# A list scheduler's port model: shorter holds for small GpSimd operations, later readers of loads

## The chip, the cores and the metric

The kernel runs on one core of a Trainium2 chip. The metric is the device time of one execution in microseconds. In the text PE is TensorE, DVE is VectorE, ACT is ScalarE, POOL is GpSimd and SP is the engine whose queue issues most transfers.

## The reference

A stack of four residual graph layers works on x of shape (128, 64, 256) with one 64x64 adjacency matrix, all in float32. Each layer takes a layer norm and a ReLU of its input.

```python
h = jnp.maximum(_layernorm(x, axis=-1), 0.0)
x = x + _L0_gnn_ref(h, adj, ...)   # two graph convolutions, then four LSTMs over windows of 1 to 4 nodes
h = jnp.maximum(_layernorm(x, axis=-1), 0.0)
x = x + _L1_gnn_ref(h, adj, adj, ...)   # spectral convolution, attention in 4 heads, MLP, three layer norms
h = jnp.maximum(_layernorm(x, axis=-1), 0.0)
x = x + _L2_gnn_ref(h, adj, ...)   # graph attention
h = jnp.maximum(_layernorm(x, axis=-1), 0.0)
x = x + _L3_gnn_ref(h, adj, ...)   # U (relu(U^T h W1 + b1)) W2 + b2, U the eigenvectors of the Laplacian
...
deg = jnp.sum(A, axis=0) + jnp.sum(A, axis=1) - jnp.diagonal(A)
L_norm = d_inv_sqrt[:, None] * L * d_inv_sqrt[None, :]
_, U = jnp.linalg.eigh(L_norm)
```

Layer 1 also needs the largest eigenvalue of its Laplacian.

## The kernel before

The 8192 rows (128 graphs of 64 nodes) are cut into tiles of 128 rows. Layer 0 takes eight groups of eight tiles; the LSTMs do most of TensorE's work, most of their products by a seven-product scheme for 2x2 blocks, whose sums of blocks GpSimd and VectorE make (`pieces`). Its results are stored to memory (`put`). Layers 1 to 3 take sixteen groups of four tiles, which are loaded from `put` one by one and stored to the output.

Beside this, the eigenvectors are computed on the core itself (`eig_decomp`, group `EIG`, its data in the tile `arena`): 62 Householder steps with 64x1, 64x64 and 64x128 operations, mostly on VectorE, each with one square root on GpSimd and, from the sixth step on, one broadcast of a matrix row by a transfer of SP's queue; then nine sweeps of multisection with 64x42 products (32 steps a sweep), a twisted factorisation, and repair of split blocks. The layers with index 1 to 3 need the result in layer 3.

Nothing of this order is written by hand. The code records every operation through proxies (`Plan.record`) with a price (`Plan.cost`: how long the engine is taken, and the latency until others may read). `Plan.schedule` then plans all engines together: again and again it picks for each engine the operation that can start first, by rank among those that are ready, and issues the earliest. The ranks of the main groups come from the group and the length of the path that follows; operations of `EIG` have the last rank on VectorE and ScalarE, and the first on TensorE and GpSimd. A value gets its buffer when its first operation is picked. `Plan.issue` emits the instructions in this order, so each engine runs its queue in the order planned, and real waits are semaphores that follow from the dependences. The planned times themselves appear nowhere on the chip.

Two parts of the plan matter here.

- **The port.** Operations marked `op.port` share one variable: all of GpSimd's, and VectorE's whose operands are all in SBUF, bar the layer norm's statistics and the reductions. Such an operation isn't planned to start before `port`, and sets it to the end of its own planned time.
- **Readiness.** When an operation is planned, those that depend on it become ready at its end plus latency, and a slack for another engine (0.05 us, for TensorE 0.12 or 0.4). A transfer of SP's queue is priced at its bytes over 390 GB/s, at least 0.6 us, with 2.2 us more until its readers may start.

`ln_stats` is the layer norm: for four tiles, eight statistics operations on VectorE, then four operations of four elements a partition on GpSimd: add epsilon, the power -0.5, a product, and a change of sign. ScalarE reads the two rows as scale and bias.

Of the kernel before, what the change touches and what calls it, by code (L numbers as in the profile page):

```python
# [8 lines left out]
ALU = mybir.AluOpType  # L9
# [59 lines left out]
class Plan:  # L69
# [44 lines left out]
    def record(self, eng, name, args, kw):  # L114
        op = self.run
        if op is None:
            op = Op(eng, name, args, kw, self.group)
            op.lead = self.lead
            if self.behind:
                op.deps.add(self.behind)  # L120
        else:
            op.calls.append((name, args, kw))
        aps = [(a, i == 0) for i, a in enumerate(args) if self.is_ap(a)]
        aps += [(a, k in ("out", "accum_out")) for k, a in kw.items() if self.is_ap(a)]
        for a, write in aps:
            ap = a.ap if isinstance(a, Virt) else a
            if str(ap.space) == "DRAM" and not self.tc.is_my_tile(ap.tensor):
                continue
            key = ap.tensor.name
            if isinstance(a, Virt):  # L130
                key = id(a.val)
                op.vals[a.val] = True
            step, count = ap.ap[0]
            p0, f0 = (ap.offset // step, ap.offset % step) if step else (0, ap.offset)
            ends = [s * (n - 1) for s, n in ap.ap[1:]]
            region = (p0, p0 + count, f0 + sum(min(e, 0) for e in ends), f0 + sum(max(e, 0) for e in ends) + 1)
            if isinstance(a, Virt) and a.val.kind in ("bank", "seed"):
                op.deps |= {o for o in a.val.users if o.eng != eng}
                a.val.users.append(op)
            reads, writes = self.seen.setdefault(key, ([], []))  # L140
            for log in (reads, writes) if write else (writes,):
                for r, o in log:
                    if o is not op and r[0] < region[1] and region[0] < r[1] and r[2] < region[3] and region[2] < r[3]:
                        op.deps.add(o)
                        if log is writes:
                            op.late.add(o)
                if write:
                    log[:] = [(r, o) for r, o in log if not (
                        region[0] <= r[0] and r[1] <= region[1] and region[2] <= r[2] and r[3] <= region[3])]
            (writes if write else reads).append((region, op))  # L150
        if eng == "PE":

            val = args[0].val
            if val.last and val.last is not op:
                op.deps.add(val.last)
            val.last = op
        if op is self.run:
            return self.link(op)
        flat = [a.ap if isinstance(a, Virt) else a for a, _ in aps]
        op.cost, op.lat = self.cost(op, flat)  # L160

        op.port = eng == "G" or (eng == "V" and not name.startswith("bn_") and "reduce" not in name
                                 and all(str(ap.space) == "SB" for ap in flat))
        op.index = len(self.ops)
        self.ops.append(op)
        self.link(op)
        if self.whole:
            self.run = op
# [9 lines left out]
    @staticmethod  # L178
    def cost(op, aps):

        def free(ap):
            n = 1
            for _, c in ap.ap[1:]:
                n *= c
            return n
        n = max(free(a) for a in aps)
        if op.name == "dma_start" and op.eng != "SP":
            return 0.6, 4.0
        if op.eng == "PE":
            n = free(aps[0])  # L190
            if op.name == "transpose":
                c = 0.11
            elif aps[0].ap[0][1] <= 64 and aps[1].ap[0][1] <= 64:
                c = 0.08
            else:
                c = 0.001672 * n + 0.006 if n >= 128 else 0.2
            return c, c + 0.22
        if op.eng == "V":
            if op.name == "bn_stats":
                c = 0.33  # L200
            elif op.name == "bn_aggr":
                c = 0.09
            elif op.name in ("tensor_copy", "tensor_scalar") and all(str(a.space) == "SB" for a in aps):
                c = 0.075 + 0.0006 * n + 0.05 * (len(aps) - 2)
            elif op.name == "reciprocal":
                c = 0.075 + 0.0065 * n
            elif op.name == "tensor_reduce" and aps[1].ap[-1][0] != 1:
                c = 0.075 + 0.0022 * n
            else:
                c = 0.075 + 0.00105 * n  # L210
            if "accum_out" in op.kw:
                c += 0.075
            return c, c + 0.12
        if op.eng == "ACT":
            c = 0.07 + 0.00082 * n + 0.1 * max(0, len(aps) - 2)
            if op.kw.get("func", op.args[2] if len(op.args) > 2 else None) is AF.Exp:
                c += 0.12
            return c, c + 0.15
        if op.eng == "G":
            c = 0.44 + 0.14 * n if op.kw.get("op") is ALU.pow else 0.12 + 0.00218 * n  # L220
            return c, c + 0.05
        c = max(0.6, free(aps[0]) * aps[0].ap[0][1] * 4e-6 / 0.39)
        return c, c + 2.2
# [6 lines left out]
    def schedule(self):  # L230
# [19 lines left out]
        table, order, span, port, many = None, [], 0.0, 0.0, False  # L250
        while len(order) < len(self.ops):
            oldest = min(left)
            best = None
            for e, ops in ready.items():
# [3 lines left out]
                for op in ops:  # L258
                    if op.group != self.aside and op.group >= oldest + self.window(oldest) + (op.eng == "SP"):
                        continue  # L260
                    t = max(now[e], op.ready, port) if op.port else max(now[e], op.ready)
# [4 lines left out]
                    for k, c in need.items():  # L266
# [4 lines left out]
                        t = max(t, times[c - 1]) if len(times) >= c + spare else None  # L271
# [12 lines left out]
            _, t, op = best  # L284
            e = op.eng
            ready[e].remove(op)
            tb = self.table(op)
            cost, lat = op.cost, op.lat
            if tb and tb != table:
                table, cost, lat = tb, cost + 1.29, lat + 1.29  # L290
            if e == "PE" and op.many != many:
                many, cost, lat = op.many, cost + 0.178, lat + 0.178
            now[e] = t + cost
            if op.port:
                port = t + cost
            end = t + lat
            for v in op.vals:
                if v.buf is None:
# [10 lines left out]
            for o in op.after:  # L309
                o.wait -= 1  # L310
                if o.eng != e:
                    o.ready = max(o.ready, end + self.slack(o))
                else:
                    o.ready = max(o.ready, end - 0.01 if op in o.late and e != "PE" else t + cost)
                if not o.wait:
                    ready[o.eng].append(o)
# [1495 lines left out]
```

## Time and profile before

| | |
|---|---|
| median of three runs | 2116.32 us (2113.99 to 2117.18) |
| the profiled execution | 2117.02 us, span 2115.2 us |
| busy: TensorE, VectorE, ScalarE, GpSimd | 2072.3, 1767.0, 1094.7, 756.6 us |
| statistics of layer norms on GpSimd: powers of 128x4 | 110, mean 1101 ns |
| transfers of 512 KB from the input, issue to landing | 29, median 5.0 us |
| granted TensorE clock | 0.997 |

Nearly all instructions carry line L347, that of the call in `Plan.issue`, so the profile is read by engine, tile and shape. Tiles keep their names without numbers: `big`, `mids`, `stat`, `bank` and `seed` (the last two in PSUM) are pools; `arena`, `sums`, `Wih` and `Whh` hold eigenvalue data or weights first and serve as more buffers later. A busy time is the union of an engine's instructions; those of TensorE overlap and their ends are modelled. A wait names the engine whose semaphore came last.

### The profile page before, as it was taken

Reading aid. Unit: us, or ns where it says so; the run is one execution under the profiler, and the core shown is the slowest. Engines: PE = TensorE matmul, PEld = TensorE weight load, DVE = VectorE, ACT = ScalarE, POOL = GpSimd, SP = SyncE. Lnnn points to the kernel's source line nnn. Section 1 sums busy time; section 2 is a strip of 40 time slices with the busy share of each in tenths; the row PEclk is TensorE's granted clock in tenths of the full one; section 3 lists DMA queues with packets and bytes.
Section 4 is the critical chain, followed back from the end, with each engine's and each line's share of the span. In section 5 each row is a group of like instructions: output and inputs, shape, how many; then the busy total and the mean of one; then the engine's idle time right before and its main releaser. Section 6 shows DMA issues by size and latency. Waiting matters only on the chain.

```text
span 2115.2 us, 48093 instructions
## 1 busy us (share of the span) xinstructions
PE 2072.3 (98%) x17924; PEld 1675.9 (79%) x17924; DVE 1767.0 (84%) x6669; ACT 1094.7 (52%) x2451; POOL 756.6 (36%) x1144
## 2 busy tenths in 40 slices
PE   8999999999999999999999999999999999999997
PEld 6688689688788788788788789877778778877775
DVE  7788888889999999999988956868779699885785
ACT  3344544534543543543444345666666567575763
POOL 6522212222201201201100215685467658663452
PEclk9999999999999999999999999999999999999999
DMA  6000100100100100100000211100000000000001
GB/s 229 1 3 13 52 3 2 62 2 2 60 1 1 61 1 2 46 1 10 32 1 21 90 49 35 62 1 22 22 21 22 21 22 22 22 2 11 1 12 51
DMA packets 44875, 57.83 MB, mean 27 GB/s; under 512 B 8929, under 2 KB 38497, under 8 KB 44641
## 3 DMA queue, kind: packets, MB, share of 16 engines
q1 hardware_dynamic: 43536, 53.71, 7.9%
q8 instruction: 141, 2.31, 0.5%
q10 hardware_dynamic: 1104, 1.05, 0.2%
q14 instruction: 94, 0.76, 0.1%
HBM read 37.53 MB, written 16.78 MB: 26 GB/s over the span
## 4 chain that ended last, share of the span: by engine, by line
PE 80%; DVE 13%; issue 2%; ACT 2%; POOL 2%; DMA 0%; SPq 0%; ACTq 0%; DVEq 0%; POOLq 0%
PE bank L347 64%; PE seed L347 16%; DVE arena L347 5%; DVE big L347 4%; DVE stat L347 2%; ACT mids L347 1%; DVE mids L347 1%; POOL stat L347 1%; DVE sums L347 1%; POOL big L347 1%; ACT big L347 0%; DMA arena<-put 0%; DVE bank L347 0%; POOL sums L347 0%; DVE seed L347 0%
## 5 line engine op out<-in xcount | busy, mean ns | idle before, releaser
L347 PE MATMUL bank<-big,Wih 128*128 128x512 f32 (+4 forms) x1802 | 554.5, 424 | 2.9 <-DVE big L347 1.9
L347 PEld LDWEIGHTS bank<-big,Wih 128*128 128x128 f32 x1802 | 314.7, 190 | 145.5 <-issue 95.5
L347 PE MATMUL bank<-big,sums 128*128 128x128 f32 (+3 forms) x2328 | 375.7, 289 | 5.2 <-DVE seed L347 2.5
L347 ACT ACTIVATE mids<-bank,bl 128x512 f32<-128x512 f32 (+2 forms) x432 | 247.2, 576 | 214.3 <-PE bank L347 195.2
L347 PEld LDWEIGHTS bank<-big,sums 128*128 128x128 f32 (+1 forms) x2328 | 298.5, 180 | 42.8 <-issue 19.6
L347 PE MATMUL bank<-big,Whh 128*128 128x128 f32 (+3 forms) x1294 | 312.3, 327 | 0.0
L347 DVE TENSOR_TENSOR arena<-arena 64x42 f32<-64x42 f32 (+6 forms) x1358 | 276.5, 231 | 18.4 <-POOL arena L347 1.2
L347 PEld LDWEIGHTS bank<-big,Whh 128*128 128x128 f32 x1294 | 214.0, 191 | 18.5 <-issue 10.5
L347 ACT ACTIVATE mids<-seed,bl 128x256 f32<-128x256 f32 (+2 forms) x192 | 102.0, 531 | 217.0 <-PE seed L347 209.0
L347 DVE TENSOR_TENSOR big<-mids 128x512 f32<-128x512 f32 (+2 forms) x256 | 151.1, 597 | 27.1 <-ACT mids L347 17.1
L347 POOL TENSOR_SCALAR stat<-stat 128x4 f32<-128x4 f32 (+1 forms) x228 | 68.4, 301 | 281.1 <-DVE stat L347 268.9
L347 PE MATMUL seed<-big,sums 128*128 128x128 f32 (+3 forms) x896 | 143.3, 291 | 0.0
L347 DVE SCALAR_TENSOR_TENSOR arena<-arena 64x1 f32<-64x1 f32 (+15 forms) x565 | 136.1, 264 | 4.5 <-POOL arena L347 1.0
L347 POOL TENSOR_TENSOR big<-big 128x128 f32<-128x128 f32 (+2 forms) x55 | 32.9, 600 | 294.6 <-DVE big L347 151.7
L347 POOL TENSOR_TENSOR stat<-stat,mhalf 128x4 f32<-128x4 f32 (+1 forms) x114 | 123.9, 1087 | 4.8
L347 ACT COPY seed<-bank 128x128 f32<-128x128 f32 (+2 forms) x192 | 54.0, 281 | 135.8 <-PE bank L347 128.5
L347 ACT ACTIVATE mids<-big 128x256 f32<-128x256 f32 (+2 forms) x176 | 89.5, 511 | 66.3 <-DVE big L347 62.1
L347 ACT COPY mids<-bank 128x256 f32<-128x256 f32 (+3 forms) x290 | 94.8, 352 | 51.9 <-PE bank L347 51.5
L347 PEld LDWEIGHTS seed<-big,sums 128*128 128x128 f32 (+1 forms) x896 | 118.4, 183 | 3.5 <-issue 0.3
L347 DVE TENSOR_SCALAR arena<-arena 64x1 f32<-64x1 f32 (+10 forms) x506 | 100.4, 206 | 7.8 <-POOL arena L347 0.5
L347 DVE TENSOR_TENSOR big<-big,mids 128x256 f32<-128x256 f32 (+2 forms) x196 | 99.0, 509 | 7.0 <-ACT mids L347 6.0
L347 PE MATMUL bank<-Wih,big 128*128 128x256 f32 x408 | 104.8, 383 | 0.0
(517 smaller groups left out, 4480.4 us busy)
## 6 DMA issues: line engine op xcount, KB each, us to landing
big<-in_x_dram SPq DMA_DIRECT2D x29, 512.0 KB, 5.0
put<-big SPq DMA_DIRECT2D x15, 512.0 KB, 3.2
big<-put SPq DMA_DIRECT2D x8, 512.0 KB, 6.4
out_dram<-big SPq DMA_DIRECT2D x16, 256.0 KB, 2.6
Wih<-in_WihT_dram SPq DMA_DIRECT2D x3, 1024.0 KB, 11.4
Whh<-in_WhhT_dram SPq DMA_DIRECT2D x3, 1024.0 KB, 12.9
arena<-put SPq DMA_DIRECT2D x3, 512.0 KB, 5.9
sums<-put SPq DMA_DIRECT2D x3, 512.0 KB, 4.3
```

What stands on the lines that cost most here:

```text
L347: getattr(self.engines[op.eng], name)(*map(real, args), **{k: real(a) for k, a in kw.items()})
```

## The change

Three edits, all in the planner. An operation with an operand of more than one free dimension, or with more than 64 elements in it, is wide and holds the port for its whole planned time as before; any other holds it for 0.06 us at most. GpSimd operations of up to 64 elements, bar the power, are priced at 0.2 us. An operation that depends on a transfer of SP's queue, on whatever other engine, is ready 1.5 us later.

```diff
         op.port = eng == "G" or (eng == "V" and not name.startswith("bn_") and "reduce" not in name
                                  and all(str(ap.space) == "SB" for ap in flat))
+        wide = max(ap.ap[-1][1] if len(ap.ap) == 2 else 65 for ap in flat) > 64
+        op.hold = op.cost if wide else 0.06
...
         if op.eng == "G":
-            c = 0.44 + 0.14 * n if op.kw.get("op") is ALU.pow else 0.12 + 0.00218 * n
+            c = 0.44 + 0.14 * n if op.kw.get("op") is ALU.pow else 0.12 + 0.00218 * n if n > 64 else 0.2
             return c, c + 0.05
...
             now[e] = t + cost
             if op.port:
-                port = t + cost
+                port = t + min(cost, op.hold)
...
                 if o.eng != e:
-                    o.ready = max(o.ready, end + self.slack(o))
+                    o.ready = max(o.ready, end + self.slack(o) + (1.5 if e == "SP" else 0.0))
```

The ranks, the windows of groups and the buffers' reserves stay as they are.

## The prediction

> **What bounds the kernel now.** I read the busy table first, then the chain that ended last, then the same busy times cut into stages (columns: stretch, its length, busy time of each engine with its instructions).
>
> ```profile
> PE 2072.3 (98%) x17924; PEld 1675.9 (79%) x17924; DVE 1767.0 (84%) x6669; ACT 1094.7 (52%) x2451; POOL 756.6 (36%) x1144
> PE 80%; DVE 13%; issue 2%; ACT 2%; POOL 2%; DMA 0%; SPq 0%; ACTq 0%; DVEq 0%; POOLq 0%
> ```
>
> ```profile
> 0.00:50.00 50.00, 44.33 (x515) 30.13 (x516) 39.39 (x165) 17.55 (x37) 34.91 (x62) 0.93 0.70 242
> 50.00:1150.00 1100.00, 1095.72 (x7573) 885.74 (x7573) 985.39 (x4305) 499.49 (x1281) 211.75 (x379) 1.00 0.06 18
> 1150.00:1350.00 200.00, 193.91 (x1585) 170.80 (x1587) 143.99 (x491) 95.07 (x231) 60.44 (x95) 1.00 0.20 62
> 1350.00:2050.00 700.00, 690.75 (x7475) 549.53 (x7466) 554.79 (x1575) 458.39 (x857) 428.34 (x577) 1.00 0.05 14
> 2050.00:2115.20 65.20, 47.61 (x798) 39.71 (x797) 43.46 (x136) 24.16 (x48) 21.20 (x33) 0.95 0.15 50
> ```
>
> TensorE bounds it everywhere but in the last 65 us. Its idle time is 5.7 us at the start, 4.3 in layer 0, 6.1 in the change of layers, 9.3 in the three later layers and 17.6 at the end: 42.9 in all. Matmul ends are modelled, so I also took the distances between the starts of neighbouring matmuls (median 429 ns for 512 columns, 216 for 256, 143 for 168, 112 for 128) and added up what exceeds them: 89 us, of which 13 before 50 us, 19 to 1150, 37 to 2050, 20 in the tail. No change of order can give more than the 76 us outside the start; VectorE has 348 us idle and can only help through those.
>
> **What the planner believed, and what the trace shows.** The planner let one variable, the port, keep VectorE's SBUF operations and GpSimd's operations apart for the whole planned length of either. The trace shows three things on that.
>
> ```profile
> L347 POOL TENSOR_SCALAR stat<-stat x228: 213/229/1378, 6.9 to 2097.3; 128x4 f32<-128x4 f32 x110, 128x2 f32<-128x2 f32 x4
> L347 POOL TENSOR_TENSOR stat<-stat,mhalf x114: 696/1037/1859, 7.2 to 2095.9; 128x4 f32<-128x4 f32 x110, 128x2 f32<-128x2 f32 x4
> L347 POOL TENSOR_TENSOR stat<-stat x114: 188/199/661, 8.0 to 2097.0; 128x4 f32<-128x4 f32 x110, 128x2 f32<-128x2 f32 x4
> ```
>
> ```profile
> 1419.98 1.38 POOL L347 TENSOR_SCALAR stat<-stat 128x4 f32<-128x4 f32 x1
> 1420.01 1.27 DVE L347 TENSOR_TENSOR big<-big,stat 128x512 f32<-128x512 f32 x2
> ```
>
> ```profile
> 666.20 1.38 DVE L347 TENSOR_TENSOR arena<-arena 64x42 f32<-64x42 f32 x4
> 666.67 1.27 POOL L347 TENSOR_TENSOR big<-big,big 128x128 f32<-128x128 f32 x3
> ```
>
> The first three rows are durations in ns (minimum, median, maximum) of the four small operations of every layer norm. In the second view two 512-wide VectorE products run beside a small GpSimd one in 1.27 us together, as fast as ever, and it is GpSimd's 229 ns operation that takes 1378. In the third, beside wide GpSimd operations, the 64x42 product takes 0.35 us on average where it takes 0.19 alone. Over the whole trace: a 512-wide product from SBUF to SBUF has a median of 681 ns with GpSimd idle and 679 ns inside a small power (41 of them); the 64x42 product 190 ns alone, 189 inside a small power, 470 inside a wide operation. So a small GpSimd operation does not delay VectorE, a wide one does, and VectorE does delay the small ones.
>
> The Trainium skill, page "SBUF — State Buffer", section "Who interferes with whom", says that a VectorE instruction with two SBUF inputs contends with a GpSimd one that reads SBUF, and that whoever comes first holds the pair for the whole instruction. The wide rows here agree; the small ones don't: 679 ns beside a power of 1037 ns is no hold. "Perfetto Trace Analysis", section "Identifying the Most-Contended Engine", warns that matmul busy time is a poor measure and names weight-load time; that is 79% here, which agrees with my counting distances. No page prices the power or these small operations; the rows above do.
>
> **The change, part by part.** No instruction, transfer or semaphore is added or removed. Only planned times change, hence the order within each engine's queue, and which buffer a value gets.
>
> *Holds.* Before, one layer norm's four operations were planned at 0.129 + 1.0 + 0.129 + 0.129 = 1.39 us of port (0.12 + 0.00218 n, and 0.44 + 0.14 n for the power). 110 of these are 153 us. The 65 powers of the eigenvalue stage at 0.58 are 38 us, its 60 small memsets at 0.12 are 7: 198 us. After, 0.06 each: 440 + 65 + 60 operations, 34 us. The planner believes 164 us more of the port. A hold costs only where VectorE had nothing else to do: small GpSimd operations last 268 us in the trace, and VectorE was busy in 205 of them, so 63 us of its 348 idle us (18%) lie beside them. As an upper end I give this share of the 76 us that TensorE loses outside the start: 13.7. Some of this idle time waits for TensorE or ScalarE anyway (the rows of waits on VectorE name them nearly always), so I take half, **7 us**; the lower end is 0. Below nothing is the slower rival.
>
> *Prices.* Small GpSimd operations go from 0.129 to 0.2 (measured medians 229 and 199), a chain from 1.39 to 1.6 planned against 229 + 1037 + 199 + 229 = 1.69. Readers on ScalarE are planned 0.2 us later; ScalarE waits for these chains 87 us in all but is 48% idle. The small memset goes from 0.12 to 0.2 though it takes 0.093. Cover: ScalarE's idle time; if gone, 0.2 us times the three chains of the tail, 0.6 us. I take 0.
>
> *Loads.* Every operation on another engine that depends on a transfer of SP's queue is planned 1.5 us later.
>
> ```profile
> big<-in_x_dram SPq DMA_DIRECT2D x29, 512.0 KB, 5.0
> big<-put SPq DMA_DIRECT2D x8, 512.0 KB, 6.4
> ```
>
> Half a megabyte was planned at 1.34 + 2.2 = 3.5 us and takes 5.0 to 6.4; it becomes 5.0. The only wait of VectorE for a load that shows is 1.6 us in its row of statistics from arena. So the gain is at most 1.6 us plus part of the 13 at the start, the loss at most 1.5 us where the first readers are put behind something else. The same 1.5 us reaches the 57 row broadcasts of the eigenvalue stage (and the writers of the matrix that they read): planned 0.6 + 2.2 = 2.8 us, measured 2.1, now 4.3. Their iterations are 7.9 us apart in the trace (109.5 to 554.1 us for 56), so 4.3 still hides; were an iteration to depend on it alone, 56 x 1.5 = 84 us of planned time would move that stage later, into the stretch after 1150 where VectorE is 72% busy. On SP's queue nothing passes anything of weight: it idles until the buffers it loads into come free. I take **0**, with -2 to +2.
>
> *Sum.* 2117.0 us (the profiled execution: span 2115.2 and 1.8 around it) - 7 = 2110. The median of the runs is 2116.3, 0.7 lower: **2109**.
>
> **Rivals.** *Nothing within 0.2%.* (0.2%, 4 us, is about what a measurement of this kernel can tell from no change; the three runs spread over 3.2.) TensorE is 98% busy and its queue only shuffles. For it: between 50 and 1150 us only 19 us are lost at all, and of the first half megabytes all but a few are loaded far ahead. It gives 2116.
>
> *Slower: the released room is filled with eigenvalue work in front of TensorE's next input.* The hold was also a reserve, since the planner's prices for VectorE are low.
>
> ```profile
> L347 DVE TENSOR_TENSOR arena<-arena 64x42 f32<-64x42 f32 x855 | 140.3, 205 | 7.2
> L347 DVE SCALAR_TENSOR_TENSOR arena<-arena 64x1 f32<-64x1 f32 x269 | 60.4, 233 | 3.8 <-POOL arena L347 1.0 <-issue 0.2
> ```
>
> The 64x42 product is planned at 0.075 + 0.00105 x 42 = 0.119 and takes 0.205 on average, which alone hides 74 us. Between 50 and 1150 us, 61 powers (35 us) and 12 layer norms (17 us) release 52 us of port; the planner fills them with eigenvalue operations, which have VectorE's lowest rank. VectorE is 90% busy there and takes its queue in order: each one too many stands before a gate product, behind it ScalarE's tanh and TensorE's next step. If half of the 52 us do so and half of that reaches TensorE, 13 us: 2129. Against it: TensorE loses so little in this stretch that it has cover of several steps. It decides once TensorE's lost time between 50 and 1150 grows from 19 to over 26, more than the 7 gained.
>
> *Slower by a little: the block turned round.* Beside two-input VectorE work the small operations take 477, 1234 and 414 ns on average (63, 35 and 23 of them), against 229, 1036 and 199 elsewhere; a chain so covered takes 2.6 us instead of today's mean of 301 x 2 + 1101 + 244 = 1.95. More VectorE work beside them means more of this: 0.65 us on each of the tail's three bare chains and on some groups before, 2 to 5 us: 2120.
>
> *It doesn't do what it says.* The test of 64 elements looks at every port operation, VectorE's own 64x1 and 64x64 ones too; they then hold GpSimd off for 0.06 instead of 0.08 to 0.14 us. That is no more than 0.1 us an operation in the plan and would leave 2116.
>
> **How the numbers follow.** Forecast, with its larger variants (up to 13.7 + 2, and the tail of 17.6 idle us, where reordering can move some 8 either way): 0.48. Nothing, by either reason: 0.24. Slower through the eigenvalue work 0.20, through the chains 0.08. A changed order moves every later choice, so signs are uncertain although each price is small. The range goes from 2116 - 13.7 - 2 - 8 = 2092 to 2129 + 2 = 2131, leaving 1 in 10 out at each end. The likeliest case's own range is 2098 to 2114.
>
> **What would show it.** Right: the same instruction counts and 98 to 99% TensorE; idle beside small GpSimd operations below 63 us; TensorE's idle time in 1150 to 2050 below 15.4 and in the tail below 17.6; the small stat operations' means up a little. Slower rival: TensorE idle in 50 to 1150 above 4.3 with waits for DVE big, seed or mids. Wrong altogether: a new wait on a load, the eigenvalue stage ending later than 1200 us with later layers waiting for it, or a changed tail outweighing all the rest.

## The result and the profile after

The changed kernel takes 2108.25 us (2106.31 to 2109.63, six runs) against 2116.32: a ratio of 0.9961, with 0.9948 to 0.9974 as its 95% interval, 8 us or 0.4% faster. The profiled execution took 2106.31 with a span of 2104.5.

The busy table and the chain of the changed kernel, to lay beside those of before:

```profile
PE 2063.7 (98%) x17924; PEld 1676.3 (80%) x17924; DVE 1771.8 (84%) x6669; ACT 1095.0 (52%) x2451; POOL 775.8 (37%) x1144
...
PE 85%; DVE 10%; ACT 2%; issue 1%; DMA 1%; POOL 0%; DVEq 0%; ACTq 0%; SPq 0%
```

The engines' instruction counts are those of before; TensorE is busy 8.6 us less for the same 17924 matmuls: delays that do not count as idle time have gone. The same stages as before (the last one ends with the span; the last three numbers of a line are the granted TensorE clock, the DMA share and GB/s):

```profile
0.00:50.00 50.00, 42.70 (x508) 28.88 (x508) 36.78 (x156) 17.11 (x38) 37.62 (x64) 0.93 0.70 242
50.00:1150.00 1100.00, 1093.50 (x7564) 885.45 (x7557) 996.73 (x4344) 498.28 (x1277) 218.16 (x374) 1.00 0.06 17
1150.00:1350.00 200.00, 195.34 (x1490) 172.06 (x1489) 139.06 (x460) 95.61 (x233) 60.69 (x97) 1.00 0.21 67
1350.00:2050.00 700.00, 692.80 (x7679) 557.01 (x7678) 561.16 (x1609) 464.55 (x869) 440.93 (x584) 1.00 0.05 15
2050.00:2104.50 54.50, 39.40 (x701) 32.87 (x700) 38.09 (x105) 19.43 (x38) 18.36 (x27) 0.99 0.17 56
```

Idle time of TensorE is 7.3, 6.5, 4.7, 7.2 and 15.1 us, 40.8 in all: only 2.1 less. The better measure is the one of the prediction, the distances between the starts of matmuls beyond their medians. It fell from 88.8 us to 79.1: at the start 13.0 to 14.0, in layer 0 19.0 to 20.3, to 2050 us 36.7 to 29.7, in the tail 20.1 to 15.1. That is 9.7 of the 10.7 us between the two spans. In all kernels below, the span less this lost time lies between 2025.1 and 2027.7 us. All have the same matmuls, so this is nearly bookkeeping: it says in which stage the time went, not why.

A part of the lost time is TensorE's clock. The traces record stretches of 3.4 or 6.8 us with a granted clock of 0.5, and matmuls of one size start in them 1.98 times as far apart as elsewhere (median). Up to the last matmul, the kernel before has 12.5 us of such stretches and the changed one 6.8; the distances within them exceed the medians by about 6.1 and 2.7 us, so some 3.4 of the 9.7 us are there, most of it in the tail: 5.7 us of such stretches before, none after.

Between 50 and 1150 us VectorE is busier by 11.3 us, and the last row broadcast of the eigenvalue stage leaves at 527.3 us instead of 554.1. The layer norm's small operations:

```profile
L349 POOL TENSOR_SCALAR stat<-stat x228: 222/231/1186, 4.5 to 2087.6; 128x4 f32<-128x4 f32 x110, 128x2 f32<-128x2 f32 x4
L349 POOL TENSOR_TENSOR stat<-stat,mhalf x114: 721/1038/2110, 4.8 to 2086.2; 128x4 f32<-128x4 f32 x110, 128x2 f32<-128x2 f32 x4
L349 POOL TENSOR_TENSOR stat<-stat x114: 191/202/1179, 5.7 to 2087.3; 128x4 f32<-128x4 f32 x110, 128x2 f32<-128x2 f32 x4
```

Medians are within 3 ns of those before. Of 273 us of small GpSimd operations VectorE now leaves 47 unused (before: 63 of 268). All this looks like the prediction's mechanism at work, and every sign that the prediction named for its forecast came true: this idle time fell below 63 us, TensorE's idle time between 1150 and 2050 from 15.4 to 11.9 and in the tail from 17.6 to 15.1, and the means of the small operations rose a little. The experiments show that these signs don't credit the mechanism with the time.

### The profile page after: what moved, and what is told of

The parts are those of the page before. It is cut to its first block, busy times and chain, and to the rows that moved or that the text cites. A ratio compares the mean times of both kernels' runs of the same rounds, so it can differ in the third digit from the quotient of the medians.

```text
span 2104.5 us, 48069 instructions
## 1 busy us (share of the span) xinstructions
PE 2063.7 (98%) x17924; PEld 1676.3 (80%) x17924; DVE 1771.8 (84%) x6669; ACT 1095.0 (52%) x2451; POOL 775.8 (37%) x1144
## 4 chain that ended last, share of the span: by engine, by line
PE 85%; DVE 10%; ACT 2%; issue 1%; DMA 1%; POOL 0%; DVEq 0%; ACTq 0%; SPq 0%
PE bank L349 69%; PE seed L349 16%; DVE big L349 3%; DVE arena L349 3%; DVE stat L349 2%; DVE sums L349 1%; DVE mids L349 1%; ACT mids L349 1%; DMA big<-in_x_dram 1%; ACT big L349 0%; DVE seed L349 0%; POOL stat L349 0%; ACT arena L349 0%; ACT sums L349 0%; ACT L349 0%
## 5 line engine op out<-in xcount | busy, mean ns | idle before, releaser
L349 PE MATMUL bank<-big,Wih 128*128 128x512 f32 (+4 forms) x1776 | 545.7, 425 | 1.1 <-DVE big L349 0.7
L349 PE MATMUL bank<-big,sums 128*128 128x128 f32 (+3 forms) x1904 | 360.4, 303 | 5.8 <-DVE big L349 2.5
L349 PEld LDWEIGHTS bank<-big,sums 128*128 128x128 f32 (+1 forms) x1904 | 285.4, 189 | 40.7 <-issue 17.7
L349 PEld LDWEIGHTS bank<-big,Whh 128*128 128x128 f32 x1274 | 210.4, 191 | 20.7 <-issue 9.8
L349 PE MATMUL seed<-big,sums 128*128 128x128 f32 (+2 forms) x768 | 139.9, 303 | 0.0
L349 DVE SCALAR_TENSOR_TENSOR arena<-arena 64x1 f32<-64x1 f32 (+16 forms) x565 | 128.7, 250 | 10.6 <-ACT arena L349 3.5
L349 POOL TENSOR_TENSOR big<-big,B1T 128x512 f32<-128x512 f32 x32 | 37.8, 1186 | 255.1 <-DVE big L349 233.8
L349 POOL MEMSET arena<- 64x2 f32 (+5 forms) x72 | 7.8, 113 | 306.2 <-DVE arena L349 301.7
L349 PEld LDWEIGHTS seed<-big,sums 128*128 128x128 f32 x768 | 114.7, 191 | 3.2
L349 DVE TENSOR_SCALAR arena<-arena 64x1 f32<-64x1 f32 (+8 forms) x506 | 103.5, 214 | 6.8 <-POOL arena L349 0.3
L349 PE MATMUL seed<-big,Whh 128*128 128x128 f32 (+3 forms) x418 | 101.7, 326 | 0.3 <-DVE big L349 0.3
```

Source lines behind the costliest of these rows:

```text
L349: getattr(self.engines[op.eng], name)(*map(real, args), **{k: real(a) for k, a in kw.items()})
```

## The experiments

Theory A is that of the prediction: the released port is the gain. Theory B: any edit of the planner draws another order, the orders scatter, and the gain belongs to the one drawn. Theory D came between them, after the first four runs: no single edit helps, but the three together do. Where an expectation gives the plan's total, this is the length of its own schedule that the planner ends with; it is no time of the chip. The ratios are against the kernel before, run on the same chip.

**One edit at a time.** The first keeps only the hold, the second only the 1.5 us, the third only the price of 0.2.

```diff
# only the hold
-            c = ... if op.kw.get("op") is ALU.pow else 0.12 + 0.00218 * n if n > 64 else 0.2
+            c = ... if op.kw.get("op") is ALU.pow else 0.12 + 0.00218 * n
-                    o.ready = max(o.ready, end + self.slack(o) + (1.5 if e == "SP" else 0.0))
+                    o.ready = max(o.ready, end + self.slack(o))
# only the loads: the line of the price put back; only the price: that of the loads; and in both
-        op.hold = op.cost if wide else 0.06
+        op.hold = op.cost
```

> Only the shorter hold of the change; prices and readers of loads as before. Theory A (the released port is the gain, as the prediction had it): nearly all of the 8 us, 2107 to 2112. Theory B (the three edits only reshuffle the order, and the chip follows the total of the plan that happens to come out): this plan's own total is 2092.1, that of the kernel before 2093.3 and of the changed one 2083.3; the chip takes 23 to 25 us more than these two, so 2115 to 2117, no gain.

Measured: 2125.49 us, ratio 1.0041 (1.0029 to 1.0054), slower. The forecast of theory A fails for this kernel; what one order says of the edit in general, the scatter below must tell. Its stages, from 50 us on:

```profile
50.00:1150.00 1100.00, 1092.90 (x7568) 881.37 (x7569) 998.84 (x4357) 498.34 (x1272) 209.28 (x374) 1.00 0.06 17
1150.00:1350.00 200.00, 192.05 (x1443) 172.90 (x1441) 130.11 (x436) 93.12 (x232) 57.19 (x93) 0.99 0.20 64
1350.00:2050.00 700.00, 691.30 (x7482) 549.71 (x7486) 554.37 (x1561) 465.06 (x857) 427.12 (x572) 1.00 0.05 15
```

VectorE's third number in the first line is 998.8, as in the changed kernel, and 130.1 in the second: eigenvalue work is pulled forward here as well (last broadcast at 514.0 us). VectorE's idle time beside small operations falls as well, to 57 us. But TensorE loses 42.3 us between 1150 and 2050, against 36.7 before and 29.7 after. Most of these 5.6 us more is a slow clock: between 1150 and 2050 this kernel runs 10.2 us at half clock, the kernel before and the changed one none, and the distances within these stretches exceed the medians by about 4.8 us. The longer of the two begins just after TensorE waited 2.17 us for ScalarE (a line of TensorE's timeline, with the wait in brackets, and then the line of the stretch):

```profile
1550.59 0.32 PE L349 MATMUL seed<-Ub,big 64*64 64x64 f32 x2 [2.17 <-ACT big L349]
1550.70:1557.50 6.80, 6.75 (x74) 5.27 (x75) 6.14 (x20) 4.47 (x12) 6.56 (x9) 0.50 0.01 2
```

So the eigenvalue work moves forward as forecast, and in this order it does not pay.

> Only the 1.5 us for readers of loads. Theory A: nothing, 2114 to 2118, since VectorE's only visible wait for a load was 1.6 us. Theory B: the plan's total is 2095.7, so 2119 to 2121, some 3 us slower than before.

Measured: 2131.99 us, ratio 1.0072 (1.0060 to 1.0085). The statistics' waits for their loads do not vanish, as VectorE's rows show, first of before, then of this kernel:

```profile
L347 DVE BATCH_NORM_STATS2 stat<-arena 128x6 f32<-128x256 f32 x48 | 17.3, 410 | 1.6 <-DMA arena<-put 1.6
```

```profile
L349 DVE BATCH_NORM_STATS2 stat<-big 128x6 f32<-128x256 f32 x252 | 91.0, 405 | 3.1 <-DMA big<-in_x_dram 2.9
```

They are 1.6 and 2.9 us, a small part of the 16 us by which the kernel is slower. TensorE lost 45.4 us between 1150 and 2050 and 16.8 at the start. It ran 25.6 us at half clock, the most of all kernels.

> Only the price of 0.2 us for small GpSimd operations. Theory A: nothing, 2115 to 2118. Theory B: the plan's total is 2103.8, so 2127 to 2129, 0.5% slower than before.

Measured: 2136.18 us, ratio 1.0097 (1.0083 to 1.0111), the worst of all, for a price that is nearer to the measured one than the old. TensorE lost 53.6 us between 1150 and 2050, where it ran 10.2 us at half clock.

**The change without its part on loads.**

```diff
-                    o.ready = max(o.ready, end + self.slack(o) + (1.5 if e == "SP" else 0.0))
+                    o.ready = max(o.ready, end + self.slack(o))
```

> The change without its part on loads: shorter holds and the new price. Theory A: the gain stays, 2107 to 2112. Theory B: the plan's total is 2096.1, so 2119 to 2121, slower than before, although the part taken out was priced at nothing.

Measured: 2120.19 us, ratio 1.0017 (1.0010 to 1.0024). The 1.5 us is worth -12 us on top of the other two and +16 alone; the three parts alone add up to 9 + 16 + 20 = +45 us, and together they give -8. Sizes that depend so on their neighbours aren't sizes of effects.

**A change without meaning.** The slack that the planner adds between engines was moved by one or two nanoseconds, in the changed kernel and in the one before.

```diff
-        return 0.05
+        return 0.049      # 0.051 and 0.052 in the others
```

> The changed kernel with the planner's slack between engines at 0.049 us instead of 0.05, which no event on the chip could tell apart. Theory D (the three edits together bring the plan nearer to the chip, so the gain belongs to them): 2105 to 2112. Theory B (a list scheduler's order scatters, and the gain belongs to this one order): anything from 2105 to 2135; the plan's total is 2083.5 against 2083.3 unperturbed, so near 2108 if the total tells, with a few us for the scatter of the chip about it.

Measured: 2107.82 us, ratio 0.9957 (0.9945 to 0.9969). It is nearly the same order: by a count (a lower bound) of the planned operations that keep their relative order in an engine's queue, it is the nearest relative of the changed kernel, so it says little by itself:

```
kept in relative order, at least, of 4902 on TensorE and 6325 on VectorE
changed kernel against slack 0.049    4500   5198
changed kernel against slack 0.052    3767   4387
kernel before against slack 0.051     4072   4600
kernel before against changed kernel  3238   3750
```

> The changed kernel with the slack at 0.052. Theory D: 2105 to 2112. Theory B: the gain is gone; the plan's total is 2097.5, and with 23 to 36 us on top of it as in the runs so far, 2120 to 2134.

Measured: 2126.91 us, ratio 1.0039 (1.0027 to 1.0052). All three edits are in it, and it is 19 us slower than the changed kernel. The expectation of theory D fails here.

> The kernel before with the slack at 0.051. Theory D: 2113 to 2119. Theory B: the kernel before is itself a good draw; total 2094.2, so 2117 to 2130.

Measured: 2124.43 us, ratio 1.0036 (1.0024 to 1.0047).

> The kernel before with the slack at 0.052. Theory D: 2113 to 2119. Theory B: total 2088.2, so 2111 to 2124: a number without meaning for the chip may by itself bring what the change brought.

Measured: 2118.02 us, ratio 1.0007 (0.9999 to 1.0015), no change. So one to two nanoseconds move the kernel before by +8 and +1 us and the changed one by 0 and +19. The 8 us of the change lie inside this scatter.

**Orders chosen by the plan's own total.** By the first eight runs, kernels whose plan was short by its own account were mostly short on the chip. Of 160 random settings of the changed planner's constants the two with the lowest totals were run, and of 100 settings of the kernel before the lowest.

```diff
# a: hold 0.08, small price 0.15, loads 1.25, slack 0.045, TensorE's slack 0.3
# b: hold 0.1, small price 0.15, loads 1.0, slack 0.06, TensorE's slack 0.3
# before, none of the three edits:
-            return 0.4 if op.group >= REST and op.group != EIG else 0.12
+            return 0.5 if op.group >= REST and op.group != EIG else 0.1
```

> The changed planner with other constants, taken as the lowest plan total of 160 random settings: hold 0.08, small price 0.15, loads 1.25, slack 0.045, slack for TensorE in the later layers 0.3. Theory B with the total as a guide: 2079.3, 4.0 below the changed kernel's, so 2102 to 2108, at or below both kernels. If the total does not guide: anything between 2108 and 2136, as the other neighbours.

Measured: 2112.37 us, ratio 0.9981 (0.9972 to 0.9990).

> The second lowest of the same 160: hold 0.1, small price 0.15, loads 1.0, slack 0.06, TensorE slack 0.3; total 2079.8. The same two expectations: 2102 to 2109, or anything up to 2136.

Measured: 2111.51 us, ratio 0.9972 (0.9963 to 0.9982). Both beat the kernel before and neither the changed one; they lie 4.4 and 2.5 us above the ranges expected.

> None of the three edits: the kernel before with two slacks moved (TensorE 0.5 in the later layers instead of 0.4, 0.1 elsewhere instead of 0.12), the lowest plan total of 100 such settings, 2087.1 against 2093.3. Theory D (the gain belongs to the edits): 2113 to 2125. Theory B with the total as a guide: 2110 to 2117, so the edits aren't needed for a part of the gain.

Measured: 2123.80 us, ratio 1.0034 (1.0022 to 1.0047). The total was 6 us lower than that of the kernel before, and the chip is 7 us slower. This lies within the range of theory D and above that of theory B with the total as a guide. The totals against the medians:

```
plan total  chip     chip - total
2093.3      2116.3   23.0   before
2083.3      2108.3   25.0   changed
2092.1      2125.5   33.4   hold only
2095.7      2132.0   36.3   loads only
2103.8      2136.2   32.4   price only
2096.1      2120.2   24.1   without loads
2083.5      2107.8   24.3   changed, slack 0.049
2097.5      2126.9   29.4   changed, slack 0.052
2094.2      2124.4   30.2   before, slack 0.051
2088.2      2118.0   29.8   before, slack 0.052
2079.3      2112.4   33.1   low total a
2079.8      2111.5   31.7   low total b
2087.1      2123.8   36.7   before, low total
```

The correlation is 0.86. The last column has a mean of 30 and a standard deviation of 4.6 us, so a plan's total tells a bad order from a good one, not two good ones. The kernel before has the lowest difference of all, and its neighbours were no faster: it seems to have been a good draw itself.

The edits may still help as a set. With all three, at the change's constants or near them, five orders were run, 2107.8 to 2126.9 us, and the four fastest of all kernels are among them; but two of these were chosen by their total and one is the changed kernel's twin. The six without the hold took 2116.3 us and more.

**Small GpSimd work by itself.** The changed kernel's own order, with three products of 128x4 into a spare tile after each layer norm chain, added when the instructions are issued and so unknown to the plan.

```diff
+                if op.eng == "G" and name == "tensor_scalar" and kw.get("op0") is ALU.mult:
+                    rs = real(args[0])
+                    for _ in range(3):
+                        self.engines["G"].tensor_tensor(self.spare[:, :rs.shape[-1]], rs, rs, op=ALU.mult)
```

> The changed kernel in exactly its own order, with three more products of 128x4 on GpSimd into a spare tile after each of the 114 layer norm chains: 342 operations of 0.20 us or more, at least 68 us of small GpSimd work that nobody waits for. If small operations do not delay VectorE (the premise of the change): VectorE's busy time within 3 us of 1772 and the time within 3 us of 2108. If they held it for their whole length (the old model): VectorE is busy with two-input SBUF work about a third of the time, so 20 us or more of added VectorE time, and 2112 or more.

Measured: 2118.75 us, ratio to the kernel before 1.0011 (1.0003 to 1.0019), so 10.5 us above the changed kernel. The added operations' group, and then the busy table:

```profile
L353 POOL TENSOR_TENSOR spare<-stat 128x4 f32<-128x4 f32 x330 | 77.5, 235 | 26.4
```

```profile
PE 2070.9 (98%) x17924; PEld 1678.1 (79%) x17924; DVE 1782.3 (84%) x6669; ACT 1094.6 (52%) x2451; POOL 854.8 (40%) x1486
```

The group shown has the 330 operations of 128x4; 12 of 128x2 make it some 80 us in all. VectorE is busier by 10.5 us, between the two expectations, and the time lies where the old model put it. (That expectation reckoned with two-input SBUF work on VectorE for a third of the time; in the trace of the changed kernel it is 975 us, 46%.) But the queues have the same order, so each of VectorE's 6669 instructions can be set against its twin. The 182 that newly lie beside small GpSimd operations take 0.1 us less in all. The 112 that newly lie beside wide ones (79 were undisturbed, 33 were beside small ones) take 16.7 more, the 107 that no longer do take 12.0 less, and 1054 that stay beside wide ones take 5.1 more. So the premise of the change holds: small operations by themselves cost VectorE nothing that shows. What they take is GpSimd's time: wide operations behind them fall on other VectorE work, and ScalarE waits longer for the layer norms. ScalarE's waits for them in the changed kernel, then in this one (total, times, longest):

```profile
ACT big L349 <- POOL stat L349: 28.0, 15, 4.4
ACT arena L349 <- POOL stat L349: 23.5, 10, 6.4
ACT mids L349 <- POOL stat L349: 18.8, 12, 7.8
ACT sums L349 <- POOL stat L349: 10.4, 6, 3.2
```

```profile
ACT big L349 <- POOL stat L349: 35.1, 20, 4.4
ACT arena L349 <- POOL stat L349: 26.8, 12, 6.5
ACT mids L349 <- POOL stat L349: 23.1, 14, 7.8
ACT sums L349 <- POOL stat L349: 14.8, 13, 3.2
```

In these four rows 80.7 us become 99.8. How much of the 10.5 us comes by the collisions and how much by these waits was not separated.

## Why the prediction was right, and where it wasn't

The number was right, 2109 against 2108.25, and the sign. That it was met so closely is luck: two nanoseconds of slack away, the same three edits give 2126.91. The reason given for it isn't borne out: with the holds released and nothing else, the kernel is slower by 9 us.

- **What bounds the kernel.** Right, and the part that carries over. TensorE is 98% busy in both, and the lost time by start distances accounts for the difference between the spans within 1 to 2 us in every kernel here. The stages were named rightly too: -7.0 us between 1150 and 2050 and -5.0 in the tail, +1.3 in layer 0 and +1.0 at the start.
- **Holds: 7 us.** The step that isn't borne out takes a share of VectorE's idle time as a share of TensorE's lost time. That VectorE leaves less unused beside small operations was right (63 us to 47, and 57 with the hold alone), and so was the premise. But with the hold alone, where 6 us less lay idle, TensorE lost 7 us more (96.1 in all against 88.8), so the one does not set the other. Whether the 7 us are right on average isn't shown.
- **Prices: 0, loads: 0.** As costs of instructions these stand: nothing was added, and VectorE's waits for loads are a few microseconds in either kernel. The statistics' waits grew from 1.6 us to 3.0; the prediction overlooked 3.0 us of waits for the adjacency matrices and biases at the start, and these fell to 0.3. As effects on the time zero was wrong: +20 and +16 alone. The prediction's sentence that a changed order moves every later choice was the true size of these steps; it should have stood in the sum as a scatter of some 8 us (the standard deviation below), not in the range alone.
- **The rival of eigenvalue work pulled forward.** Its first half is the steadiest trace of the change: VectorE is busy for 990 to 1005 us between 50 and 1150 in all eight kernels that release the hold, and for 978 to 986 in the six that don't. Its second half, that TensorE pays for this, is small: layer 0 lost 20.3 us after and 20.7 with the hold alone, against 19.0, below the 26 named as deciding. The other sign named for this rival did show in the changed kernel: TensorE's idle time there rose from 4.3 to 6.5 us, and its waits for VectorE's `arena`, the eigenvalue work, from 0.8 to 2.7. Of all kernels only the changed one with slack 0.052 went beyond the 26, to 28.3, and it is one of the slow ones.
- **The block turned round.** Small operations remain stretched beside two-input VectorE work: the sign change and the addition of epsilon take 466 ns there on average (70 of them) and 231 beside statistics and PSUM work. The means of 128x4 rose from 301 to 306 ns, for the powers from 1101 to 1123 and for the products from 244 to 287, so a chain takes 2.02 us instead of 1.95. This is far below the 2.6 of a chain that is covered all along; its share in the time wasn't measured.
- **The test of 64 elements.** The prediction dismissed its reach to VectorE's own operations at no more than 0.1 us each. It left out the sum: in the changed planner 2386 small VectorE operations hold the port for 125 us less in all, beside 164 for GpSimd's. No run keeps one without the other, so which of the two drew the new order is open.
- **"Wrong altogether" would have been a tail outweighing the rest.** The tail gave 5.0 of the 9.7 us, as much as the balance of all the rest, so by this sign the forecast was at the edge of being wrong. The tails of all kernels lay between 14.8 and 21.8.

Whether the released hold is worth anything on average stays open. Leaving out the orders chosen by total, and the twin of the changed kernel, four with it average 2120.2 us and five without it 2125.4, with a standard deviation of 8.5 us in each; that doesn't decide it.

## What to carry to other kernels

A list scheduler's output is one draw: before crediting an edit of its model, move a constant that means nothing by 2 to 4% in both versions and see how far the time goes; here up to 19 us, against a gain of 8. When one engine is 98% busy, sum the distances between its starts beyond their medians, stage by stage, since that sum held nearly the whole difference between fourteen kernels and shows where to look; then see how much of it is waiting and how much a lowered clock. Judge a model's correction by its footprint in the trace as well (here eigenvalue work moved forward), and when a lucky order is kept, keep it as an order, not as proof of the model.

## What the runs showed of the hardware

In these traces, GpSimd's small operations and VectorE's two-input operations from SBUF disturb each other on one side only. A power of 128x4 that takes 1.04 us leaves a 512-wide VectorE product beside it at 679 ns (681 alone), while a 229 ns operation of the layer norm took 477 on average beside such products (63 of them), and 1378 at most. Wide GpSimd operations do cost VectorE: SBUF operations that overlap them took 115 us more in the kernel before than their undisturbed medians, and those that overlap small ones 0.4 us less. And some 80 us of small work that no one waits for, on an engine that is 37% busy, cost 10.5 us of the whole.

In these traces, TensorE's granted clock halves for stretches of 3.4 or 6.8 us, and matmuls then start 1.98 times as far apart. Most of these stretches begin during or within a few microseconds after TensorE sat idle for some 1 to 4 us in all (2.17 us in the lines shown). The fourteen kernels spent between 6.8 and 25.6 us in such stretches up to their last matmul; the three with one edit alone had 22.0 to 25.6, and the changed kernel and its twin 6.8.
